# Products on a constant tile before the first transposes, and the first sequence's features in two halves

## The chip, the cores and the metric

The kernel runs on one core of a Trainium2 chip. The core has five engines with queues of their own: TensorE (PE, with its weight loads shown as PEld), VectorE (DVE), ScalarE (ACT), GpSimd (POOL) and SyncE (SP, which here only issues loads and stores). The metric is the device time of one execution in microseconds (us). Lower is better. Of several runs the median counts.

## The reference

The input x has 4 sequences of 512 tokens with 256 features, in 32-bit floating point, as everything here. What is computed, in short:

```
x = x + layernorm(attn(layernorm(x)))
x = x + layernorm(ffn(layernorm(x)))

attn(x):  q = silu(x @ Wq1 @ Wq2);  k1 = x @ Wk1 @ Wk2;  v = x @ Wv
          a = sigmoid(sigmoid(k1));  k = 1 - a
          h[t] = a[t] * h[t-1] + k[t] * v[t]          # a scan along the tokens
          out = q * h, scaled by the root mean square of its 512 features, times norm_w
          return out @ Wo
ffn(x):   six blocks of  x = gelu(x @ W1.T + b1) @ W2.T + b2 + x
          with a layernorm with gain and bias between blocks
```

Wq1 and Wk1 are 256x128, Wq2 and Wk2 128x512, Wv 256x512, Wo 512x256; the hidden size of the blocks is 1024.

## The kernel before, in words

**Tiling.** A tile of x has 128 tokens on the partitions and 256 features; a sequence b has four, `xs[b][0..3]`. Products want the features on the partitions, so the normalized tiles `n` are transposed: `to_features` (L647) transposes the four tiles of a sequence for one half d of the features (128 of 256) into one bank `pt`, and ACT copies the bank to a tile of 128 x 512 tokens. `Attention.features(d)` (L684) does that for d = 0 and 1 and puts the two results, from the ring `tcs`, in `self.xt`. The ring `pts` has two banks, the pool `banks` six.

**The head of the program.** An identity for the transposes is built on POOL (`make_identity`), two constants (`neg_half`, `ones`) are set on DVE, and ACT runs an activation on `ones`. The four tiles of the first sequence are loaded by SP and ACT in turns, then the weights. `first_norm` (L673) normalizes the first sequence in two pairs of tiles: statistics on DVE (`token_stats`, L609), the reciprocal root on POOL (`rstd_of`, L619, two steps for a pair), and the scaling on DVE (`centred`, L640). Then come `features(0)` and `features(1)`, and the loop over the sequences.

**One sequence.** `k1_q1` (L697) forms the two inner products (x @ Wk1 and x @ Wq1, `inner`, L689) of 128 x 512, each the sum of two products over d, and copies them from their bank. For each e of four groups of 128 value features, `value(e)` (L702) forms v, and `scan(e)` (L707) the outer products with Wk2 and Wq2, three sigmoids on ACT, two elementwise operations and the scan itself on DVE, and the product with q on POOL. The outputs of one sequence (`output`, L743, and `residual`, L757, which uses products with `ones`) are interleaved with the scans of the next. Then the six blocks run over two groups of two sequences, with products on 256 tokens whose operands are sums of blocks (`sa`, `tx`, `sb`) formed on POOL. `txs` are 18 tiles of 128 x 256 that hold such sums of the input; they are written first when the features of the first two sequences for the blocks are complete.

**What sets the order.** Every operation is not issued at once but entered into a plan (`Plan.op`, L244) with its engine, an estimated cost, and the buffers that it reads and writes. `Plan.latest` (L264) goes backwards through the plan and gives each operation a due time; `Plan.run` (L281) then plays the engines forward in time by the costs, and each engine takes, of the operations that are ready, the one that is due first. The order that results is the order of instructions in each engine's queue. So a changed cost, or other buffers, can move instructions far away. A product's cost is stated in `product` (L486):

```python
0.858 * rhs.size / 512 if rhs.size > 1 else 0.12,
```

A moving operand of one column occurs only in the products with `ones`; the others have 256 or 512. Outside of the plan, and so ahead of it in each queue, stand the identity, the constants and the activation on `ones`.

**In the profile** all products have line L491, all transposes L502, elementwise operations of two tensors L457, those with scalars L471, copies on ACT L442 and activations L440, loads L512. Statistics are L614 and L615. A product of 32-bit operands is recorded as two matrix instructions and two weight loads, a transpose as one of each.

## Time and profile before

| | |
|---|---|
| median of 3 runs | 725.82 us (725.61 to 726.36) |
| the profiled execution, its own time | 725.47 us |
| its span, from first to last instruction | 723.7 us |
| PE busy | 707.5 us, 98% of the span |
| DVE, ACT, POOL busy | 58%, 53%, 69% |
| four tiles of the first sequence landed | 2.92, 3.26, 3.64, 4.75 us |
| wq1, wk1, wk2, wq2, wv landed | 6.12, 6.42, 6.84, 7.52, 9.24 us |
| x of the third sequence landed, last tile | 14.79 us |
| first transpose, first product | 5.83, 8.75 us |
| last transpose of the program begins | 714.1 us |

Times in the views are us from the start of the span unless marked ns. A line of the timeline gives the start, the length, the engine, the line of the kernel, the operation, what it writes and reads, its size and how many instructions are merged; in brackets stands how long the engine was idle before it, and what ended the wait. A name such as `bank<-tc,xt` leaves the buffers' numbers out; `tc` and `xt` are the tiles' own names, so that wq1 and wk1, which lie in memory that is lent from tiles of the name `xt`, appear under it, and the other weights of the head under `w`. The chain lines give start, length and place. The profiled execution is one run: sums are made against its 725.47 us.

### The profile page before, as it was taken

The page shows a single profiled execution, that of the slowest core. Times are in us where ns is not written, and L with a number is a line of the kernel's source. Part 1 is how long each engine was busy: PE and PEld are TensorE (multiplying, and loading weights), DVE is VectorE, ACT ScalarE, POOL GpSimd, SP SyncE. Part 2 cuts the span into 40 slices and gives each one's busy share as a digit, 9 for nine tenths or more (in the row PEclk, how much of TensorE's full clock was granted, in tenths as well). Part 3 has the DMA queues.
Part 4 walks back from the last instruction along what each step waited for, and adds up shares of the span by engine and source line. Part 5 has one row for each costly group of instructions (what it writes and reads, how often), then busy time and mean ns, then how long its engine had stood idle before and what let it go on. Part 6 is the DMA issues. An engine that isn't in the chain of part 4 may idle for free.

```text
span 723.7 us, 8185 instructions
## 1 busy us (share of the span) xinstructions
PE 707.5 (98%) x2672; PEld 467.6 (65%) x2672; DVE 418.5 (58%) x824; ACT 384.9 (53%) x667; POOL 500.7 (69%) x664
## 2 busy tenths in 40 slices
PE   6999999999999999999999999999999999999994
PEld 3465568757658568477576585684775765865853
DVE  4556555936827629449268277284493592672855
ACT  2847766735726627437447266175374472661732
POOL 4897668695884668863958846778639589366363
PEclk9999999999999999999999999999999999999997
DMA  8200001000110001010001100001100000100001
GB/s 257 79 1 0 1 2 57 2 0 0 59 59 2 0 1 29 31 58 1 0 1 60 40 19 0 1 6 54 59 1 1 0 1 20 40 0 1 30 23 65
DMA packets 14922, 19.18 MB, mean 26 GB/s; under 512 B 1568, under 2 KB 12832, under 8 KB 14880
## 3 DMA queue, kind: packets, MB, share of 16 engines
q1 hardware_dynamic: 14048, 17.74, 7.5%
q10 hardware_dynamic: 832, 0.92, 0.4%
q8 instruction: 21, 0.34, 0.2%
q14 instruction: 21, 0.17, 0.1%
HBM read 16.56 MB, written 2.10 MB: 26 GB/s over the span
## 4 chain that ended last, share of the span: by engine, by line
PE 96%; DVE 1%; ACT 1%; POOL 1%; DMA 0%; issue 0%; POOLq 0%; ACTq 0%
PE bank L491 86%; PE pt L502 6%; PE pt L491 4%; DMA x<-in_x 0%; DVE st L614 0%; POOL r L457 0%; DVE n L481 0%; DVE mv L615 0%; DVE tmp L457 0%; POOL r L471 0%; ACT tmp L442 0%; ACT n L440 0%; DVE ht L457 0%; ACT L534 0%; ACT tc L442 0%
## 5 line engine op out<-in xcount | busy, mean ns | idle before, releaser
L442 ACT COPY tmp<-bank 128x512 f32<-128x512 f32 x144 | 84.2, 585 | 187.4 <-PE bank L491 175.4
L457 POOL TENSOR_TENSOR tc<-ht,tc 128x512 f32<-128x512 f32 x96 | 120.6, 1274 | 73.6 <-DVE st L614 38.1
L491 PE MATMUL bank<-tx,sa 128*128 128x256 f32 x672 | 161.3, 380 | 0.2 <-DVE tmp L457 0.2
L491 PEld LDWEIGHTS bank<-tx,sa 128*128 128x128 f32 x672 | 125.2, 190 | 26.7 <-issue 9.2
L481 DVE SCALAR_TENSOR_TENSOR tmp<-bank,b,xt 128x512 f32<-128x512 f32 x48 | 36.0, 750 | 152.5 <-PE bank L491 152.5
L457 DVE TENSOR_TENSOR ht<-tmp,bank 128x512 f32<-128x512 f32 x156 | 100.9, 679 | 29.0 <-ACT tmp L442 25.6
L440 ACT ACTIVATE ht<-ht,b 128x512 f32<-128x512 f32 x144 | 99.3, 715 | 16.7 <-DVE ht L457 16.7
L491 PE MATMUL bank<-tc,w 128*128 128x512 f32 x224 | 101.6, 593 | 0.0
L491 PE MATMUL bank<-tc,sb 128*128 128x512 f32 (+1 forms) x200 | 90.1, 576 | 0.0
L491 PE MATMUL bank<-ht,sb 128*128 128x512 f32 (+1 forms) x200 | 88.3, 575 | 0.0
L491 PE MATMUL bank<-ht,w 128*128 128x512 f32 x192 | 86.2, 593 | 0.0
L457 DVE TENSOR_TENSOR tmp<-tmp,bank 128x512 f32<-128x512 f32 x96 | 64.8, 678 | 20.8 <-ACT tmp L442 10.4
L457 POOL TENSOR_TENSOR tx<-xt,tx 128x256 f32<-128x256 f32 x108 | 75.1, 730 | 1.0
L491 PEld LDWEIGHTS bank<-tc,w 128*128 128x128 f32 x224 | 42.2, 190 | 40.8 <-issue 38.2
L491 PEld LDWEIGHTS bank<-ht,sb 128*128 128x128 f32 x200 | 38.0, 190 | 34.9 <-issue 33.4
L440 ACT ACTIVATE n<-sm,r 128x256 f32<-128x256 f32 x104 | 54.3, 590 | 11.2 <-POOL r L457 11.2
L491 PEld LDWEIGHTS bank<-ht,w 128*128 128x128 f32 x192 | 35.7, 190 | 35.5 <-issue 32.2
L457 DVE TENSOR_TENSOR tmp<-bank,tmp 128x512 f32<-128x512 f32 (+1 forms) x54 | 35.9, 667 | 34.4 <-PE bank L491 33.9
L471 POOL TENSOR_SCALAR r<-mv 128x4 f32<-128x4 f32 (+1 forms) x72 | 20.9, 290 | 48.4 <-DVE mv L615 44.5
L502 PEld LDWEIGHTS pt<-ident,n 128*128 128x128 f32 x224 | 29.0, 144 | 38.6 <-issue 25.6
L440 ACT ACTIVATE xt<-pt,be,g 128x512 f32<-128x512 f32 x40 | 31.1, 777 | 38.9 <-PE pt L502 38.6
L491 PE MATMUL bank<-xt,sa 128*128 128x256 f32 x192 | 51.3, 379 | 0.0
(69 smaller groups left out, 1061.6 us busy)
## 6 DMA issues: line engine op xcount, KB each, us to landing
w<-in_w1t SPq DMA_DIRECT2D x6, 1024.0 KB, 4.8
w<-in_w2t SPq DMA_DIRECT2D x6, 1024.0 KB, 5.6
out<-n SPq DMA_DIRECT2D x16, 128.0 KB, 1.7
x<-in_x SPq DMA_DIRECT2D x14, 128.0 KB, 3.4
w<-in_wv ACTq DMA_DIRECT2D x1, 512.0 KB, 5.6
xt<-in_wo SPq DMA_DIRECT2D x4, 128.0 KB, 3.6
x<-in_x ACTq DMA_DIRECT2D x2, 128.0 KB, 2.9
w<-in_wk SPq DMA_DIRECT2D x1, 256.0 KB, 4.8
```

What stands on the lines that cost most here:

```text
L440: lambda: nc.scalar.activation(dst.ap, src.ap, func, **kw)
L442: else nc.scalar.copy(dst.ap, src.ap),
L457: lambda: on(engine).tensor_tensor(dst.ap, a.ap, b.ap, alu),
L471: lambda: on(engine).tensor_scalar(dst.ap, src.ap, *by, op0, **kw),
L481: lambda: nc.vector.scalar_tensor_tensor(dst.ap, a.ap, by, b.ap, op0, op1),
L491: lambda: nc.tensor.matmul(dst.ap, lhs.ap, rhs.ap, start=start, stop=True, skip_group_check=True),
L502: lambda: nc.tensor.transpose(dst.ap, src.ap, ident.ap),
```

## The change

At the head of the program one tile of `txs`, the last, is set to 1.0 on DVE ahead of the other constants, and six products of 256 columns are issued on it, outside of the plan. They write to a bank that nothing reads. Two more such products, of 128 columns each, are entered into the plan after `k1_q1` of the first sequence, with the second normalized tile as what they wait for.

The first sequence's features are formed by `first_features(half)` instead of `features(d)`: for each half of the tokens (two tiles of 128) and each d, two transposes into 256 columns of a bank `pt` and one ACT copy of 128 x 256 into one of the tiles `txs[0..3]`. `self.xt[d]` becomes a list of parts, and `projected` forms a product part by part: over both d on the first half's columns of the bank, then on the second's. It serves `inner` and `value`. For the other sequences there is one part, as before.

The planner's cost of a product is now at least 0.224, which changes it for the products with `ones` alone.

```diff
+WARM = 6
+FILL = 2
...
-            0.858 * rhs.size / 512 if rhs.size > 1 else 0.12,
+            max(0.858 * rhs.size / 512, 0.224),
...
+    nothing, unread = txs[-1], banks.free[-1]
+    nc.vector.memset(nothing.ap, 1.0)
+
+    def warm(n):
+        nc.tensor.matmul(
+            unread.ap[:, :n], nothing.ap[:, :P], nothing.ap[:, :n], start=True, stop=True
+        )
+
+    for _ in range(WARM):
+        warm(2 * P)
     make_identity(nc, ident.ap)
     nc.vector.memset(neg_half.ap, -0.5)
     nc.vector.memset(ones.ap, 1.0)
...
-        pt = pts.next()
+        pt = pts.next()[:, : len(srcs) * P]
...
             xt = tcs.next()
             to_features(self.n, d, xt)
-            self.xt.append(xt)
+            self.xt.append([xt])
+
+        def first_features(self, half):
+
+            for d in range(ND):
+                xt = txs[2 * half + d][:]
+                to_features(self.n[2 * half : 2 * half + 2], d, xt)
+                if half == 0:
+                    self.xt.append([])
+                self.xt[d].append(xt)
+
+        def projected(self, w):
+
+            bank, at = banks.next(), 0
+            for parts in zip(*self.xt):
+                part = bank[:, at : at + parts[0].size]
+                for d in range(ND):
+                    product(part, w[d], parts[d], at == d == 0)
+                at += parts[0].size
+            return bank
 
         def inner(self, w1):
-            bank, h = banks.next(), tcs.next()
-            for d in range(ND):
-                product(bank, w1[:, d, :], self.xt[d], d == 0)
+            bank, h = self.projected([w1[:, d, :] for d in range(ND)]), tcs.next()
             act(h, bank)
...
         def value(self, e):
-            self.psv = banks.next()
-            for d in range(ND):
-                product(self.psv, wv_s[:, d, ts(e, P)], self.xt[d], d == 0)
+            self.psv = self.projected([wv_s[:, d, ts(e, P)] for d in range(ND)])
...
-    att[0].features(0)
-    att[0].features(1)
+    att[0].first_features(0)
+    att[0].first_features(1)
     for b in range(B):
         one = att[b]
         past = att[b - 1] if b else None
         one.k1_q1()
+        if b == 0:
+            for _ in range(FILL):
+                plan.op("PE", 0.43, lambda: warm(P), [one.n[1]], [unread])
```

## The prediction

> **What bounds the kernel now.** I read the first and fourth parts of the page first. TensorE (PE) is busy for 98% of the span, and the chain that ended last lies on it:

> ```profile
> PE 96%; DVE 1%; ACT 1%; POOL 1%; DMA 0%; issue 0%; POOLq 0%; ACTq 0%
> ```

> Time can only come out of what PE does, or out of stretches where it waits. The timeline of PE alone has few: none from 8.75 us until 127.8 us, where a product starts 0.4 us late at 128.44 (0.54 us with the slower records around it), and none after that until the last transposes at 713 us. So whatever PE gains before 8.75, or in the speed of its first products, reaches the end unless a new wait takes it back. The head, from the timeline of PE from 5 to 16 us (start, length, group):

> ```profile
> 5.83 1.12 PE L502 MATMUL pt<-ident,n 128*128 128x128 f32 x4 [5.83 <-DVE n L471]
> 7.17 1.12 PE L502 MATMUL pt<-ident,n 128*128 128x128 f32 x4 [0.23 <-DVE n L471]
> 8.75 5.85 PE L491 MATMUL bank<-tc,xt 128*128 128x512 f32 x8 [0.46 <-ACT tc L442]
> ```

> One product is two records, so x8 is four products (k1 and q1). The weight loads beside them give the pace, as one starts with each record:

> ```profile
> 11.47 0.34 PEld L491 LDWEIGHTS bank<-tc,xt 128*128 128x128 f32 x1 [0.52 <-issue]
> 12.32 0.34 PEld L491 LDWEIGHTS bank<-tc,xt 128*128 128x128 f32 x1 [0.52 <-issue]
> 13.15 0.19 PEld L491 LDWEIGHTS bank<-tc,xt 128*128 128x128 f32 x1 [0.49 <-issue]
> 13.58 0.19 PEld L491 LDWEIGHTS bank<-tc,xt 128*128 128x128 f32 x1 [0.24 <-issue]
> ```

> Until 13.1 us a 512-column record takes 0.85 us, afterwards 0.43: PE runs at half speed first. (The clock column reads full speed there, but the trace has no clock record before 13.1.) The chain up to 8.75 says what the first product waits for:

> ```profile
> 1.35 3.40 DMA x<-in_x
> 4.77 0.44 DVE st L614
> ...
> 7.17 0.92 PE pt L502 x3
> 8.09 0.02 issue
> 8.11 0.59 ACT tc L442
> 8.71 0.04 issue
> 8.75 17.87 PE bank L491 x36
> ```

> The fourth tile of x lands at 4.75, its normalized tile is ready at 7.44, and a 128x512 copy stands between the last transpose and the first product.

> [...] the rise at 13.1 and the fall at 716.25 (granted clock 1.00 before, 0.50 after) lie 703.15 us apart[...]. [...]

> **The change, part by part.** The mark for the sum is the end of value(0), the fourth group of the first sequence: 16.15 us before.

> (1) *Warm products.* Six products of 256 columns, two records each, half of 0.85 = 0.43 us per record cold: 12 x 0.43 = 5.1 us, from about 1.2 (they wait only for a memset) to 6.3 us. PE is idle there today until 5.83. [...] So the clock rises at 4.6 to 8.0, instead of 12.2 to 15.6 [...]. [...] If they run cold to the end, the transposes of tiles 0 and 1 begin at 6.3 instead of 5.83; tiles 2 and 3 are later anyway. Cost nothing.

> (2) *The memset.* It stands first on DVE, ahead of ones. ACT's queue has the activation on ones ahead of its loads: ones ends at 0.88, ACT's first load is issued at 0.92. The trace has no memset of 256 columns: [...] the nearest 256-column DVE row takes 0.41. I take 0.3. Tile 1 has 0.3 us of slack before DVE reads it, tile 3 none: it lands at 5.05 instead of 4.75, its normalized tile is ready at 7.75. Bounds: 0 if the activation does not hold the loads; 0.9 if tile 3 falls behind the load of wq1, issued at 1.61, of the same size. The weights have cover: wk1, wq1, wk2, wq2 land at 6.1 to 7.5; wv at 9.24, needed at 11.6.

> (3) *Fills.* Two products of 128 columns between the two pairs of tiles: 0.43 us warm, 0.85 cold, in a hole that today runs from 6.7 to 7.17 and would be 6.8 to 7.5. Cover complete when warm; cold, 0 to 0.4.

> (4) *Halves.* Four copies of 256 columns (0.36 us, the rows of the copies to sm) instead of two of 0.59; the order view shows tiles 2 and 3 transposed for d=0, then the first half's k1 product, then d=1. So the 0.59 copy leaves the path: at 7.9 the transpose of tile 3 is done and k1 starts on the first half, copied by 7.5. From there at full clock: 8 products of 256 columns at 2 x 0.216 = 3.46, two transposes 0.22, value(0) 4 x 0.432 = 1.73: the mark comes at 7.9 + 5.4 = 13.3. Splitting costs 5 ns a product (0.432 twice 0.216 against 0.429): 0.06 in all. Gain: 16.15 - 13.3 = 2.85 us.

> (5) *Order.* The planner's price of a product on ones goes from 0.12 to 0.224, and two tiles of the tc ring are no longer taken. SP's order is unchanged. POOL swaps sums of w1 with products of the scan from 20 to 60 us; those it delays are first read by PE at 37.8, about 4.5 us after they end. At 124 to 138 us more moves: on POOL four steps of an rstd (0.23 + 1.04 + 0.23 + 0.20 = 1.7 us) go ahead of the residual's; on ACT four normalizations (2.1 us) go ahead of it, into a hole of 2.09 us that ends at 130.89; on DVE a statistics pair (0.6 us) goes ahead of a bank's release and of the r that the residual waits for. ACT's copies behind them, which free banks for PE, come up to 1.6 us later, with about 1.5 us to spare. I take 0.2 us; bounds -0.5 (today's wait gone) to +1.5.

> Sum: -2.85 + 0.03 (splits after the mark) + 0.2 = -2.6 on the profiled execution's 725.47 (span 723.7): 722.85. That execution lies 0.35 under the median 725.82. [...] Forecast for the median: 722.9, or -2.9 us, -0.40%.

> **Rivals.** (a) As summed, with the clock full by 8 us: 722.9, 722.0 to 723.7; chance 0.67. For it: [...] PE has no waits downstream.

> (b) The clock comes late or is lost again. [...] With warm products, transposes and fills cold until 8.1, the mark comes at 14.5 to 15.3, so 724.0 to 724.9. [...] 724.3; chance 0.23.

> (c) The loads: tile 3 lands 0.9 late, with the order costing 1.5: 724.7, within 0.2% of before only if both meet; chance 0.06.

> (d) Slower: the reordering at 124 to 138 us. The rstd on POOL (1.7), the four normalizations on ACT (2.1) and the statistics on DVE (0.6) are in front of the copies and releases PE waits for; exposed one after another they make 4.4 us, 725.47 - 2.8 + 4.4 = 727.1. It decides from 2.9 us of new PE waits on, and measurably from 4.4. Against it: ACT has the 2.09 us hole and PE waits 0.54 us there now. Chance 0.04.

> That the products do not lift the clock at all is the late end of (b): then (4) alone is left, k1 starting 0.65 to 0.85 us earlier, and fills and transposes that close the holes.

> **Numbers.** A measurement of this kernel tells about 0.2% from no change: 1.45 us, so 724.37 divides faster from same. Faster holds (a) and over half of (b), and a bit of (c): 0.84; slower (d), 0.03 beyond 0.2%; the rest, 0.13, is same. The range runs from 721.9 (no cost in (2), today's wait gone in (5)) to 724.8 (the late ends of (b) and (c)).

> **What would show it.** Right: on PE six groups from 1.2 us, weight loads at 0.19 from 8 us or before, k1 starting at 7.9 or so, value(0) done near 13.3, no new PE idle at 120 to 140 us. Step (2): ACT's first load at 1.2 and tile 3's statistics at about 5.1. Wrong: weight loads of 0.34 beyond 9 us (b); PE waiting on ACT or DVE for over 1 us near 130 us (d); a median above 724.4.

## The result, and the profile after

| | before | after |
|---|---|---|
| median (runs) | 725.72 us (6: 724.69 to 726.36) | 722.67 us (6: 722.56 to 723.35) |
| profiled execution, span | 725.47, 723.7 us | 722.72, 720.8 us |
| first record of PE's granted clock, 1.00, begins at | 13.11 us | 6.79 us |
| first product of k1 starts | 8.75 us | 8.25 us |
| value(0) done (the mark) | 16.15 us | 13.76 us |
| from the mark to the last transposes | 697.95 us | 697.52 us |

The ratio of the times is 0.9961 with a 95% interval of 0.9949 to 0.9974: faster by 0.4%, against a forecast of 722.9. PE still sets the end; in the chain of the page its share grew by a point. From the page of the kernel after:

```profile
PE 97%; DMA 1%; DVE 1%; POOL 0%; ACT 0%; issue 0%; ACTq 0%; POOLq 0%
```

The span is 2.83 us shorter, and two stretches hold all of it: 16.15 - 13.76 = 2.40 before the mark (with unrounded ends) and 697.95 - 697.52 = 0.43 after it. The head of the kernel after, from its timeline from 0 to 16 us:

```profile
0.84 0.27 DVE L534 MEMSET tx<- 128x256 f32 x1 [0.84 <-PEq L1229]
...
1.17 5.49 PE L537 MATMUL bank<-tx 128*128 128x256 f32 x12 [1.17 <-DVE ones L545]
1.19 0.88 ACTq L514 DMA_DIRECT2D x<-in_x  x2
...
2.08 0.47 SPq L514 DMA_DIRECT2D w<-in_wk  x1
2.10 0.48 ACTq L514 DMA_DIRECT2D xt<-in_wk  x1
...
4.07 0.43 DVE L627 BATCH_NORM_STATS2 st<-x 128x6 f32<-128x256 f32 x1 [0.58 <-DMA x<-in_x]
...
6.45 0.77 PE L504 MATMUL pt<-ident,n 128*128 128x128 f32 x4
...
7.06 0.61 PE L537 MATMUL bank<-tx 128*128 128x128 f32 x4
...
7.57 0.47 PE L504 MATMUL pt<-ident,n 128*128 128x128 f32 x2
...
8.25 0.30 PEld L493 LDWEIGHTS bank<-tx,xt 128*128 128x128 f32 x2 [0.40 <-DMA xt<-in_wk]
8.25 0.70 PE L493 MATMUL bank<-tx,xt 128*128 128x256 f32 x2 [0.21 <-DMA xt<-in_wk]
```

Read from the top: the large memset takes 0.27 us ahead of `ones`, so ACT's first load is issued at 1.19 instead of 0.92. The six products (12 records) fill PE until 6.45, where the first transposes begin at once. The statistics of tile 1 wait for its landing. The first k1 product is stopped by a load, and the bracket names it: `xt<-in_wk`, which is wk1. The wait is 0.40 us on the weight load; on PE it shows as 0.21, because the modelled ends of the transposes before it reach into it. The chain of waits from 0 to 30 us says the same from the other side:

```profile
2.10 6.11 DMA xt<-in_wk
8.21 0.04 issue
8.25 0.70 PE bank L493 x2
```

Before, this chain went through the fourth tile of x and an ACT copy; now one weight's load, 6.11 us from issue to landing, is the last to arrive.

The granted clock, from busy time in stretches that end or begin where the clock record changes; their length, 3.41 us, is the distance between the three changes recorded in e9_three_ahead, an experiment below (4.12, 7.53 and 10.95 us). The columns are length, PE, PEld, DVE, ACT, POOL busy in us with their instructions, clock, DMA share, GB/s; as in the kernel before, the clock column reads 1.00 where no record exists yet, here before 6.79:

```profile
3.38:6.79 3.41, 3.41 (x10) 2.46 (x9) 2.44 (x9) 0.00 (x0) 1.81 (x4) 1.00 0.99 290
6.79:10.20 3.41, 3.20 (x20) 2.68 (x19) 1.34 (x4) 1.39 (x4) 0.09 (x1) 1.00 0.97 334
```

The stretch before the rise holds 3.41 us of PE, with the products and the first transposes; the next one, with the fills and transposes, holds 3.20, and the record stays at 1.00 until 713.35 us. The pace says the same: the twelve records of 256 columns on the constant tile take 5.28 us, 0.44 each, and the fourteen of the same size from 9.01 to 12.03 take 0.22 each.

The place near 127.8 us, where PE lost 0.54 us before, is at 124.75 in the kernel after, and PE runs through it (timeline of PE; first line before, second after):

```profile
128.44 1.75 PE L491 MATMUL bank<-tx,sa 128*128 128x256 f32 x7 [0.22 <-DVE tmp L457]
124.75 2.84 PE L493 MATMUL bank<-tx,sa 128*128 128x256 f32 x12
```

### The profile page after: what moved, and what is told of

It reads as the page before. It is cut to its first block, busy times and chain, and to the rows that moved or that the text cites. A ratio compares the mean times of both kernels' runs of the same rounds, so it can differ in the third digit from the quotient of the medians.

```text
span 720.8 us, 8269 instructions
## 1 busy us (share of the span) xinstructions
PE 710.0 (98%) x2712; PEld 474.8 (66%) x2712; DVE 419.4 (58%) x825; ACT 385.1 (53%) x669; POOL 500.3 (69%) x664
## 4 chain that ended last, share of the span: by engine, by line
PE 97%; DMA 1%; DVE 1%; POOL 0%; ACT 0%; issue 0%; ACTq 0%; POOLq 0%
PE bank L493 87%; PE pt L504 6%; PE pt L493 4%; DMA xt<-in_wk 1%; DVE st L627 0%; DVE n L483 0%; POOL r L459 0%; ACT n L442 0%; POOL r L473 0%; DVE mv L628 0%; ACT L547 0%; DVE tmp L459 0%; ACTq L514 0%; POOLq L1241 0%; PE bank L504 0%
## 5 line engine op out<-in xcount | busy, mean ns | idle before, releaser
L442 ACT ACTIVATE ht<-ht,b 128x512 f32<-128x512 f32 x144 | 99.4, 715 | 17.6 <-DVE ht L459 17.6
L493 PE MATMUL bank<-tc,w 128*128 128x512 f32 x208 | 95.0, 592 | 0.0
L493 PEld LDWEIGHTS bank<-tc,w 128*128 128x128 f32 x208 | 39.1, 190 | 35.8 <-issue 33.2
L442 ACT ACTIVATE n<-sm,r 128x256 f32<-128x256 f32 x104 | 54.1, 590 | 9.1 <-POOL r L459 9.1
L493 PE MATMUL bank<-tx,w 128*128 128x256 f32 x224 | 56.8, 379 | 0.0
L442 ACT ACTIVATE xt<-pt,be,g 128x512 f32<-128x512 f32 x40 | 31.1, 777 | 38.8 <-PE pt L504 37.9
```

Source lines behind the costliest of these rows:

```text
L442: lambda: nc.scalar.activation(dst.ap, src.ap, func, **kw)
L493: lambda: nc.tensor.matmul(dst.ap, lhs.ap, rhs.ap, start=start, stop=True, skip_group_check=True),
```

## The experiments

The readings from each one's profiled execution, beside the median of its runs (all in us):

| kernel | clock rises | k1 starts | mark | mark to last transposes | profiled | median | ratio to before, interval |
|---|---|---|---|---|---|---|---|
| before | 13.11 | 8.75 | 16.15 | 697.95 | 725.47 | 725.72 | |
| e5_cost_only | 13.85 | 9.11 | 16.70 | 697.49 | 725.57 | 725.04 | 1.0001 [0.9992, 1.0009] |
| e9_three_ahead | 4.12, 10.95 | 8.05 | 14.97 | 697.51 | 723.85 | 724.57 | 0.9989 [0.9982, 0.9995] |
| e11_twelve | 5.60 | 9.87 | 15.27 | 697.51 | 724.13 | 724.06 | 0.9982 [0.9975, 0.9989] |
| e2_halves_only | 10.09 | 7.79 | 14.44 | 697.53 | 723.57 | 723.41 | 0.9982 [0.9974, 0.9989] |
| e1_warm_only | 7.18 | 8.75 | 13.97 | 697.95 | 723.30 | 723.34 | 0.9977 [0.9970, 0.9985] |
| e7_five_no_fill | 6.32 | 8.07 | 13.58 | 697.52 | 722.84 | 722.81 | 0.9967 [0.9954, 0.9979] |
| after | 6.79 | 8.25 | 13.76 | 697.52 | 722.72 | 722.67 | 0.9961 [0.9949, 0.9974] |
| e6_no_fill | 6.93 | 7.83 | 13.34 | 697.52 | 722.38 | 722.56 | 0.9962 [0.9950, 0.9974] |
| e8_transposes_ahead | 4.50 | 7.70 | 13.10 | 697.52 | 721.98 | 722.43 | 0.9959 [0.9946, 0.9972] |
| e3_ones_first | 7.18 | 8.06 | 13.46 | 697.89 | 722.70 | 722.18 | 0.9963 [0.9951, 0.9976] |
| e10_best | 4.19 | 7.26 | 12.78 | 697.53 | 721.67 | 721.67 | 0.9948 [0.9936, 0.9961] |

The ratios are against runs of before on the same chip; medians of different experiments, taken on different chips, compare less well than the ratios: the kernel before has a median of 725.72 in the first row, and of 725.08, 725.43 and 725.43 beside the experiments.

The marks come from one execution each, and loads that are issued at the same moment land at different ones: the fourth tile of x is issued at 1.31 to 1.33 us in e3, e6, e7, e10 and e11, and lands at 3.97, 4.83, 5.47, 4.14 and 4.07. So a few tenths between two marks are not a result by themselves.

**The warm products alone (e1_warm_only).** The kernel before with the memset and the six products, nothing else.

```diff
+WARM = 6
...
+    nothing, unread = txs[-1], banks.free[-1]
+    nc.vector.memset(nothing.ap, 1.0)
...
+    for _ in range(WARM):
+        warm(2 * P)
```

> The kernel before with the memset and the six products ahead of the first transposes alone; no fills, features not halved, the order of all queues as before. Theory A (an early clock is the larger part of the gain): the clock rises by 8 us, weight loads of 0.19 from the first k1 product on, which starts at 8.7 to 8.9 us (the fourth tile's normalization, two transposes, a 0.59 us copy); value(0) ends near 14.0 instead of 16.15, the stop of PE near 126 us stays; 723.5 us. Theory B (the halves do it, since they close the holes and the clock would rise by itself): value(0) ends at 15 or later, 725 us or more.

Measured: 723.34 us (723.20 to 723.70, 15 runs); the mark at 13.97, as expected. The first k1 product starts at 8.75, just as before, and yet the mark is 2.18 earlier: all of that is the clock, half of the 4.36 us from 8.75 to 13.11 in which the kernel before ran at 0.85 us a record instead of 0.43. That the starts agree is a coincidence. It is not the copy that stops k1 here, as the expectation had it: the first copy ends at 8.45, and wk1, issued at 2.10 as in after, lands only at 8.61. The wait behind the products on `ones` is still there (second line):

```profile
8.75 3.67 PE L492 MATMUL bank<-tc,xt 128*128 128x512 f32 x8 [0.81 <-DMA xt<-in_wk]
...
126.27 1.97 PE L492 MATMUL bank<-tx,sa 128*128 128x256 f32 x8 [0.22 <-DVE tmp L458]
```

The runs of before on the same chip spread over 2.3 us (723.95 to 726.25, 38 runs), those of this kernel over 0.5. Whether the clock accounts for that is not shown: a trace of it exists for one execution of each alone.

**The halves alone (e2_halves_only).** The kernel after without memset, products and fills.

```diff
-WARM = 6
-FILL = 2
+WARM = 0
+FILL = 0
...
-    nc.vector.memset(nothing.ap, 1.0)
```

> The changed kernel without the memset, the six products and the two fills: the halves and the order are left. Theory A: k1 starts near 7.8 us, but at half clock; the rise comes [...] at 10.6 to 14 us; value(0) ends at 15.0 to 16.0; the stop of PE near 126 us is gone; 724.6 us. Theory B: the rise comes by 9.7, value(0) ends by 14; 723 us.

Measured: 723.41 us (722.74 to 725.24, 16 runs), and the mark at 14.44, better than theory A had it; the clock rises at 10.09, between the two theories. In this profile k1 starts 0.96 us earlier than before, on its first half, at half clock (its first two records take 1.06 us, in e3, past the rise, 0.60), and close to the transposes. The stretch from 6.67 to 10.09, at whose end the clock rises, holds 3.10 us of PE:

```profile
6.67:10.09 3.42, 3.10 (x11) 2.31 (x10) 1.58 (x5) 1.39 (x4) 0.28 (x1) 1.00 0.99 333
```

In the kernel before the corresponding stretch, 6.28 to 9.70, held 2.73 us of PE, and the clock rose at 13.11. So closing the holes was worth a start 0.96 us earlier and, in this execution, a rise 3.02 us earlier; its runs spread over 2.5 us, and when the clock rose in the others is not on record. The two parts alone give 0.23% and 0.18%, together 0.41%; the whole change gives 0.39%. In the times they add up within the intervals, which are wide (0.15% is 1.1 us). In the profiled heads they don't: the mark is 2.18 and 1.71 us earlier with one part, 2.40 with both. In both the clock rises earlier, at 7.18 and 10.09 instead of 13.11 (from the start of k1 to the mark it takes 7.40 us before, 5.22 in e1, 6.65 in e2 and 5.51 in after), and what one has brought the other can't bring again; in after the load of wk1 costs 0.40 on top.

**The planner's price alone (e5_cost_only).** The kernel before with one edit:

```diff
-            0.858 * rhs.size / 512 if rhs.size > 1 else 0.12,
+            max(0.858 * rhs.size / 512, 0.224),
```

> The kernel before with the planner's cost of the products on ones at 0.224 instead of 0.12, and nothing else: only the order changes, near 120 to 140 us above all. Theory A (the other order takes away the stop of PE at 127.8 us): the head is as before, no late product near 126 us, 0.5 us less: 725.2 us. Rival (the stop goes because the head is earlier, or because two tiles fewer are taken from the ring): it stays, 725.7 us.

Measured: 725.04 us (723.94 to 725.64, 13 runs), no difference from before that the interval shows; 0.5 us less, 0.07%, would lie inside it. In the trace the wait is gone (timeline of PE of this kernel, from 125 us),

```profile
127.67 2.62 PE L491 MATMUL bank<-tx,sa 128*128 128x256 f32 x11
```

and from the mark to the last transposes it takes 697.49 instead of 697.95. So the price, not the halves or the earlier head, removed those 0.46 us: with the old price e1 keeps them (697.95), with the new one e2 and after lose them. In the times this drowns in the spread of the runs, 1.7 us (its profile had the rise of the clock at 13.85 and the mark at 16.70). Which of the moved steps does it is not shown.

**The small memset first (e3_ones_first).** The kernel after, with `ones` set ahead of the large tile:

```diff
+    nc.vector.memset(ones.ap, 1.0)
     nc.vector.memset(nothing.ap, 1.0)
...
-    nc.vector.memset(ones.ap, 1.0)
```

> The changed kernel with the memset of ones moved ahead of that of the products' tile on DVE. Theory A (the larger memset holds ones, the activation on ones holds ACT's loads, and those hold the second tile of x and wk1): ACT's first load is issued at 0.92 instead of 1.19, the second tile lands at 3.3 instead of 4.05 and wk1 near 6.4 instead of 8.2, k1 starts at 7.9 instead of 8.25, value(0) ends at 13.3 instead of 13.76; 722.2 us. Rival (the DMA engines are full in any case, and the landing of wk1 is a matter of chance): wk1 lands at 7.5 or later, value(0) ends at 13.6 or later; 722.7 us.

Measured: 722.18 us (721.64 to 722.70, 5 runs). ACT's first load goes out at 0.89, tile 1 lands at 3.27 (after: 4.05) and tile 3 at 3.97 (4.84), wk1 at 7.53 (8.21). k1 starts at 8.06, only 0.19 earlier, because now PE itself is late: it has products until 6.49, transposes, mostly ahead of the rise at 7.18 (0.95 us for four, in e11, past the rise, 0.60), until 7.27 and the fills until 7.79 (timeline of PE of this kernel).

```profile
6.49 0.95 PE L504 MATMUL pt<-ident,n 128*128 128x128 f32 x4
7.27 0.61 PE L538 MATMUL bank<-tx 128*128 128x128 f32 x4
7.79 0.44 PE L504 MATMUL pt<-ident,n 128*128 128x128 f32 x2
8.06 0.60 PE L493 MATMUL bank<-tx,xt 128*128 128x256 f32 x2
```

Theory A is right about the order (ACT's load, tile 1), but wk1 came to 7.53 and not to 6.4, which is the rival's sign: the moment of ACT's issue is only part of what sets it. The rival's reason, DMA engines that are full in any case, is not shown: in e3 their share from 3.77 to 7.18 us was 0.82. The ratio lies inside the interval of after's, so in the times the two are not told apart. The profile also has a small wait of PE before 28.4 us that no other kernel shows (697.89 in the table). Its chain of waits goes back through ACT to POOL, where two sums of the first W1 stand in the way, and from these to the load of that W1, issued at 15.13 and landed at 23.32 us (after: 14.49 and 22.36).

**No fills, and five products (e6_no_fill, e7_five_no_fill).** Both from e3_ones_first:

```diff
-FILL = 2
+FILL = 0
```

and for the second also

```diff
-WARM = 6
+WARM = 5
```

> e3_ones_first without the two fills. Theory A (in e3 the loads no longer hold PE; its own added work does: the six products end at 6.48, the fills push the transposes of tiles 2 and 3 to 7.79 although the tiles are ready at 6.8 and 7.13): the transposes of tiles 2 and 3 begin at 7.3, k1 at 7.5 to 7.7, value(0) ends at 13.0 instead of 13.46; the clock still rises by 8 us; 721.8 us. Rival [...]: weight loads of 0.34 beyond 8 us, 723 us or more in some runs.

> e3_ones_first with five products ahead instead of six, and without fills. Theory A: the products end at 5.6, the first transposes start at 5.8, k1 starts at 7.5; [...] 722.0 us median with a wider spread than e6. Rival ([...] a hole doesn't matter): 721.7 us in all runs.

Measured: 722.56 us (722.38 to 722.96, 5 runs) and 722.81 us (721.75 to 724.97, 6 runs). By their medians neither reached what theory A forecast. With six products the fills bring nothing that can be measured; k1 starts at 7.83 without them and at 8.06 with them, not at 7.5 to 7.7. What holds it without fills is the ring `pts`: it has two banks, both hold the first half, and the transposes of the second half wait until ACT has copied one of them (timeline of PE of e6):

```profile
7.66 0.33 PE L504 MATMUL pt<-ident,n 128*128 128x128 f32 x1 [0.35 <-ACT tx L444]
```

With five, one execution of six took 724.97, where the other five took 721.75 to 723.32. What that execution's clock did is not on record. In the profiled one k1 starts at 8.07, and its chain of waits begins with the fourth tile of x, which lands at 5.47. In the profile of the five stands the stretch with the least PE, of those in the heads here, through which the clock stayed at 1.00 (second line):

```profile
2.91:6.32 3.41, 2.93 (x7) 1.76 (x6) 2.39 (x9) 0.00 (x0) 1.06 (x3) 1.00 0.97 273
6.32:9.73 3.41, 2.56 (x15) 2.03 (x16) 1.98 (x7) 1.29 (x4) 0.93 (x2) 1.00 1.00 345
```

The clock rose at 6.32, after 2.93 us of PE, and stayed through the 2.56 us of the next stretch, less than the 2.73 at whose end, at 9.70, it did not rise in the kernel before.

**Transposes instead of products (e8_transposes_ahead).** The kernel after with

```diff
-    for _ in range(WARM):
-        warm(2 * P)
...
+    for _ in range(4 * WARM):
+        nc.tensor.transpose(unread.ap[:, :P], nothing.ap[:, :P], ident.ap)
```

after the identity is made.

> The changed kernel with 24 transposes of 128 columns of the constant tile in place of the six products, about the same 5.1 us of TensorE time. Theory A (transposes count as busy): the clock rises by 8 us as with products; value(0) ends near 13.8; 722.7 us. Theory B (they don't): it rises [...] at 9.5 to 12 us; value(0) ends at 14.5 or later; 723.5 us or more.

Measured: 722.43 us (721.98 to 722.83, 4 runs), and the clock rises at 4.50 us, after a stretch in which PE did nothing but transposes (timeline, then busy time):

```profile
1.35 4.36 PE L543 MATMUL bank<-ident,tx 128*128 128x128 f32 x24 [1.35 <-POOL ident masks.py:199]
6.18 0.76 PE L504 MATMUL pt<-ident,n 128*128 128x128 f32 x4 [0.47 <-DVE n L473]
```

```profile
1.09:4.50 3.41, 3.15 (x15) 3.15 (x16) 1.23 (x8) 1.12 (x2) 0.20 (x1) 1.00 0.81 221
```

That is theory A: 3.15 us of transposes went ahead of the rise, and no product. The 24 also end at 5.71, so PE is free when tile 0 is ready. Not all of the earlier mark (13.10 against 13.76) is theirs: wk1, issued at 2.11, happened to land at 7.08 here, 1.13 earlier than in after.

**Three products (e9_three_ahead).** The kernel after with `WARM = 3`.

> The changed kernel with three products ahead instead of six (2.6 us, to 3.8 us; then PE is idle for some 2 us). Theory A [...]: the rise comes [...] at 9.4 to 12.8 us, as in e2_halves_only; value(0) ends at 14.4 to 15.5; 723.5 us. Rival [...]: rise by 8 us, 722.5 us.

Measured: 724.57 us (723.29 to 726.24, 20 runs), most of the gain gone and the spread at 2.95 us. Three stretches of the profiled execution:

```profile
0.71:4.12 3.41, 2.93 (x6) 1.85 (x6) 1.19 (x6) 1.49 (x2) 0.50 (x2) 1.00 0.66 188
4.12:7.53 3.41, 1.41 (x10) 1.08 (x10) 2.79 (x10) 0.65 (x2) 1.91 (x4) 1.00 0.96 276
7.53:10.95 3.42, 3.31 (x10) 2.46 (x10) 1.16 (x5) 0.74 (x2) 0.00 (x0) 0.50 0.87 291
```

The three products made 2.93 us of PE in the first, and the clock rose at 4.12, its end. In the next PE was idle for 2.02 us without a break and had 1.41 us of work; at 7.53 the clock fell (0.50 in the third line's clock column) and stayed there until 10.95. A k1 record of 256 columns took up to 0.80 us there, and 0.38 at 1.00. In this execution the early rise, 2.67 us ahead of after's, did not last until the work arrived, and the mark came at 14.97 instead of 13.76.

**The sum of the best (e10_best).** From e8: `ones` ahead of the large memset, and no fills.

```diff
-FILL = 2
+FILL = 0
...
+    nc.vector.memset(ones.ap, 1.0)
     nc.vector.memset(nothing.ap, 1.0)
...
-    nc.vector.memset(ones.ap, 1.0)
```

> Changed kernel with the memset of ones ahead of the large one, 24 transposes of the constant tile in place of its six products, and no fills. If the two gains of the separate kernels add up (the ones ahead: scalar engine's loads at 0.89 instead of 1.19 us; the transposes end at 5.7 instead of 6.45 us, so that the sequence's own transposes don't queue behind them), the first product of k1 starts at 7.4 to 7.7 us, value(0) ends at 12.8 to 13.1 and the median is 722.0 (721.6 to 722.5). If the load of wk[0] sets the start whatever is issued earlier, it starts at 7.7 as with the transposes alone and the median is 722.4.

Measured: 721.67 us (721.58 to 722.56, 5 runs), the lowest of all; k1 starts at 7.26, earlier than expected, and the mark is at 12.78. Between the first transpose of the constant tile and k1, PE is idle for at most 0.43 us at a time (timeline of PE of this kernel):

```profile
1.35 4.21 PE L544 MATMUL bank<-ident,tx 128*128 128x128 f32 x24 [1.35 <-POOL ident masks.py:199]
5.98 0.76 PE L504 MATMUL pt<-ident,n 128*128 128x128 f32 x4 [0.43 <-DVE n L473]
7.11 0.31 PE L504 MATMUL pt<-ident,n 128*128 128x128 f32 x1 [0.37 <-ACT tx L444]
7.26 0.60 PE L493 MATMUL bank<-tx,xt 128*128 128x256 f32 x2
```

Its ratio of 0.9948 [0.9936, 0.9961] is against before; beside after's 0.9961 [0.9949, 0.9974] the intervals overlap, and the two were timed on different chips, so that it is faster than after is not shown by the times. Its mark says why it should be, 12.78 against 13.76. What stands last before k1 is again the copy that frees a bank of `pts` (third line), as in e6.

**Twelve products (e11_twelve).** e3_ones_first with `WARM = 12`.

> Changed kernel with the memset of ones ahead and twelve products on the constant tile instead of six. If the full clock is all that counts [...], the six more products cost only their own time on TensorE's queue: some at half clock until about 7 us, the rest 0.43 us each at full clock, together 2.2 us; the first transposes start near 8.7, value(0) ends near 15.6, and the median is 724.4 (723.9 to 724.9), slower than with six by 2 us. If the transposes' cover hid them (other engines still had to bring the tiles), the loss would be under 1 us, and the median 723.0.

Measured: 724.06 us (723.49 to 725.01, 20 runs); the first transposes start at 8.64 instead of 6.49. The mark is 1.81 us later than with six (e3), and by the ratios, 0.9982 against 0.9963, the time is 1.4 us longer. The clock rises at 5.60; the six more products cost their own time, 2.15 us, since the tiles are ready before (in e3 the first two at 6.10).

## Why the prediction was right

The sum was -2.85 at the head, and -2.6 in all; the trace has -2.40 at the head, -0.43 behind it, and -2.83 of span. The total is close because two errors of opposite sign met, 0.45 too much at the head and 0.63 too little for the order; that they nearly cancel is luck. That the median would come out at the profiled execution's 722.85 and not, as before, 0.35 above it was the author's estimate; measured, that execution took 722.72 and the median is 722.67.

(1) *Warm products*: right. Full clock at 6.79, within the 4.6 to 8.0 given. Those bounds, and the 12.2 to 15.6 beside them, were the author's estimate: how much work goes ahead of a rise the trace of the kernel before, with one rise at 13.11, does not show. e1 has 2.18 us from this part alone. "Cost nothing" held only because the tiles and wk1 were late too: with tiles ready earlier (e3, e6) the six products' end at 6.49 becomes a limit of its own.

(2) *The memset*: the duration was right (0.3 assumed, 0.27 measured), the place was not. The step named tile 3, with no slack, as what suffers, and said that "the weights have cover". Tile 3 landed at 4.84, 0.09 later than before; tile 1 landed 0.79 later, past its 0.3 us of slack; and wk1 landed at 8.21 instead of 6.42. That one was counted as covered, and it was the one that stopped PE, for 0.40 us beyond the tiles. Working from issue times alone failed here. Before, ACT issues wk1 at 1.83, ahead of SP's wk2 at 2.08; after, at 2.10, just behind it. In the profiles with wk1 issued at 1.8 it took 4.6 to 5.7 us to land (before, e2, e3, e5, e6, e7, e10, e11), with it issued at 2.1 it took 5.0 to 6.5 (after, e1, e8, e9). That the larger wk2 ahead of it is the reason is not shown, and e9 speaks against it: there wk1 is issued at 2.09, ahead of wk2 at 2.12, and still took 5.9. What the four profiles with the later issue share is that wq1, from SP, lands at 4.7 to 4.8 instead of 5.6 to 7.2: there wk1 lands later and wq1 earlier. Why wk1 lands so late stays open.

(3) *Fills*: they ran at full clock from 7.06, beside waits that were there anyway. In after they cost nothing, because wk1 came later still; that with six products ahead they bring nothing is what e6 shows against e3, where the mark is 0.12 earlier without them, too little to count. The part of the step that they close a hole was right; that the clock needs them was not stated, and in e6 it rose at 6.93 and stayed without them.

(4) *Halves*: right in kind. From the start of k1 to the mark it took 5.51 us against 5.41 in the sum; the 0.10 lies between the start of the first k1 product and the transposes behind it (0.54 instead of 0.43). The start came at 8.25 and not 7.9; without the 0.40 of (2) it would have been 7.85.

(5) *Order*: the sign was wrong. The term was +0.2 (bounds -0.5 to +1.5); it measured -0.43, almost the lower bound, with the wait at 127.8 gone. The step argued from which steps moved ahead of which, and put a price on the exposed ones; none of those prices shows as a wait of PE. Every kernel with the new price has 697.49 to 697.53 from the mark to the last transposes, e3 apart.

Of the rivals, (b), a clock that comes late or is lost again, did not happen in after's profile, and none of its six runs took over 723.35; in e9 the clock was lost, at 7.53, after a stretch with 1.41 us of PE. (c) had the right mechanism, a load, but the load was wk1 and cost 0.40. (d) did not occur: there is no new wait of PE from 120 to 140 us.

## What to carry to other kernels

When PE has nothing to do at the start, fill it with work on a constant tile until just before the real work is ready, and try both sides of that amount. Here three products left PE idle for 2.02 us and the clock fell back to 0.50 from 7.53 to 10.95 (e9); twelve held the first transposes until 8.64 instead of 6.49 (e11). The runs came to lie closer as well: over 2.3 us before, over 0.5 with the six products alone (e1). Set the smallest constant first if an issuing queue waits for it: with 0.27 us of memset ahead of `ones`, ACT's loads went out 0.27 us later and wk1 landed at 7.1 to 8.6 us in four profiles, against 6.4 to 7.5 in the eight others. When a critical input comes earlier, look at every other input of the first instruction again: a load that had 2.3 us of slack became the last to arrive.
